# Zero matmuls ahead of the first tile, an earlier second tile, a later bias broadcast and a shorter scale chain in a gated layer kernel on one core

## The chip, the cores and the metric

The kernel runs on one core of a Trainium2 chip. The metric is the device time of one execution in microseconds (us), lower is better. Times given as "us" come from executions on the chip; positions such as "at 7.75" are microseconds from the start of the span of one profiled execution.

## What is computed

For 1024 tokens (4 x 256) of width 512 the layer normalises each token, runs a gated projection in which half of the entries of each row are dropped, runs a mixture of experts with a shared expert, and multiplies the two:

```
xn = layernorm(x)                                  # 1024 x 512, eps 1e-5
s  = silu(xn @ w_gate.T)                           # 1024 x 1376
s[the 688 entries of smallest |s| in each row] = 0
s  = (s * (xn @ w_up.T)) @ w_down.T                # 1024 x 512
logits = xn @ router_w + router_b                  # 16 experts in 4 groups
scores = softmax(logits) + router_bias             # best 2 groups, then best 2 experts
y  = sum over chosen experts of score * ((silu(xn@w1+b1) * (xn@w2+b2)) @ w3 + b3)
z  = (silu(xn@sw1+sb1) * (xn@sw2+sb2)) @ sw3 + sb3 # the shared expert, inner width 256
out = x + s * silu(y + z)
```

All data are float32.

## The kernel before, in words

The entry function runs `quick_path` and, only if a flag is set at its end, `general_path`. The profile is of an execution that ran `quick_path` alone, so only that one matters here.

Tokens are cut into 8 tiles of 128, one token per partition. The 1376 columns of the gate and up projections are cut into three blocks (512, 512 and 352; `COLS`), the 512 of the contraction into four chunks of 128. In the trace each matmul call of float32 data appears as two MATMUL instructions and two weight loads, so one block of one tile (four chunks) is eight instructions.

The start of `quick_path`, which the change touches, goes as follows:

- SP, the queue for plain loads, issues tile 0 of x (`load_x`, L516), then the four row chunks of the first block of gate weights (L527), then tiles 1, 2 and 3 of x, then the other two blocks of gate weights (L531) and the router weights (L532). Tiles 4 to 7 follow in a later loop; they reuse the four buffers of tag "x", so each waits until an earlier tile was normalised. After them come the shared expert's weights (L940, L941) and the up weights (L946).
- POOL builds the identity matrix for the transposes and issues four loads on its own queue: router bias terms, the experts' bias columns, and `b3s_sb` (L544), the shared expert's output bias, 512 values broadcast to 128 partitions. It is read by `finish` at L890, first at 149.3.
- `stats(t0, n)` handles n tiles on VectorE (DVE). Per tile it takes BATCH_NORM_STATS (L568) and its aggregation (L569); then, for all n tiles at once, it forms the reciprocal square root: add eps (L574), two integer instructions for a first guess (L576, L577), and three Newton steps of four small instructions each (L580 to L583). Below, "scale chain" means L574 to L583, fifteen instructions, each needing the one before it.
- `normalise(t0, n)` writes `xn` (DVE, L588), transposes it on TensorE in four chunks into `pt` (L593), and ScalarE copies `pt` to `xnT` (L594).
- `gate(t, k)` multiplies `xnT` of tile t by column block k (L608) into `pz`; ScalarE applies silu (L615).

The program calls these for tile 0, for tile 1, and for tiles 2 and 3 together:

```
for t, n in ((0, 1), (1, 1), (2, 2)):
    stats(t, n)
    normalise(t, n)
    for j in range(t, t + n):
        gate(j, 0)
```

The order of instructions on each engine is not that of the text: a planner in the framework takes them by priority, which follows the program, but fills an engine's gaps with later instructions that it believes to be ready by its own estimate of times. In the trace VectorE starts its instructions in the order of its list, so one placed early whose data come late holds up what stands behind it.

After the start come the other gate blocks, the search for each row's median magnitude (DVE and ScalarE), the choice of experts, the shared expert, the up projection, the fetched experts, and per tile `finish`: expert outputs, transposes of s, the down projection (L921), product and residual.

Of the kernel before, what the change touches and what calls it, by code (L numbers as in the profile page):

```python
# [9 lines left out]
F32 = mybir.dt.float32  # L10
# [4 lines left out]
ALU = mybir.AluOpType  # L15
# [4 lines left out]
P = 128  # L20
H = 512
# [7 lines left out]
E = 16  # L29
# [452 lines left out]
def quick_path(  # L482
# [15 lines left out]
    nc = tc.nc  # L498
    NT = N_TOK // P

    const = ctx.enter_context(tc.tile_pool(name="const", bufs=1))
# [8 lines left out]
    def psum(name):  # L510
        return ps.tile([P, 512], F32, tag="mm", name=name)


    def load_x(t, again=""):
        xt = work.tile([P, H], F32, tag="x", name=f"x{again}{t}", bufs=4)
        nc.sync.dma_start(xt, x[ts(t, P), :])  # L516
        return xt
# [6 lines left out]
    X = {0: load_x(0)}  # L524
    lo, n = COLS[0]
    for c in range(HC):
        nc.sync.dma_start(wg_sb[:, c, :n], wg[ts(c, P), :n])  # L527
    for t in range(1, 4):
        X[t] = load_x(t)
    for lo, n in COLS[1:]:  # L530
        nc.sync.dma_start(wg_sb[:, :, lo : lo + n], wg_v[:, :, lo : lo + n])  # L531
    nc.sync.dma_start(wg_sb[:, :, I:], rw)  # L532


    ident = const.tile([P, P], F32, tag="ident", name="ident")
# [4 lines left out]
    nc.gpsimd.dma_start(rbias_sb, rbias.partition_broadcast(P))  # L540
    bcols_sb = const.tile([P, 2 * NCH], F32, tag="bcols", name="bcols_sb")
    nc.gpsimd.dma_start(bcols_sb, bcols)
    b3s_sb = const.tile([P, H], F32, tag="b3s", name="b3s_sb")
    nc.gpsimd.dma_start(b3s_sb, b3[E].partition_broadcast(P))  # L544
    ones = const.tile([P, P], F32, tag="ones", name="ones")
    nc.gpsimd.memset(ones, 1.0)

# [17 lines left out]
    def stats(t0, n):  # L565
        for t in range(t0, t0 + n):
            st = small.tile([P, 6], F32, tag="st", name=f"st{t}")
            nc.vector.bn_stats(st, X[t])  # L568
            nc.vector.bn_aggr(mv[:, t, :], st)  # L569


        r = rstd[:, t0 : t0 + n]
        ve = small.tile([P, n], F32, tag="ve", name=f"ve{t0}")
        nc.vector.tensor_single_scalar(ve, mv[:, t0 : t0 + n, 1], EPS, ALU.add)  # L574
        ri = r.bitcast(I32)
        nc.vector.tensor_single_scalar(ri, ve.bitcast(I32), 1, ALU.logical_shift_right)  # L576
        nc.vector.tensor_scalar(ri, ri, -1.0, float(0x5F3759DF), ALU.mult, ALU.add)  # L577
        q = small.tile([P, n], F32, tag="q", name=f"q{t0}")
        for _ in range(3):
            nc.vector.tensor_mul(q, r, r)  # L580
            nc.vector.tensor_mul(q, q, ve)
            nc.vector.tensor_scalar(q, q, -0.5, 1.5, ALU.mult, ALU.add)
            nc.vector.tensor_mul(r, r, q)  # L583

# [345 lines left out]
# [4 lines that stand above are left out]
            gate(j, 0)  # L934
    for t in range(4, NT):
        X[t] = load_x(t)
    shared = []
    for e in range(E, NCH):
        w = expert_tiles(f"shared{e}")
# [5 lines left out]
    for lo, n in COLS:  # L945
        nc.sync.dma_start(wu_sb[:, :, lo : lo + n], wu_v[:, :, lo : lo + n])  # L946
    stats(4, 4)
    for k in range(1, 3):
        for t in range(4):
# [53 lines left out]
def swiglu_topk_gated_by_moe_kernel(  # L1003
    tc: tile.TileContext,
    x: bass.AP,
    wg: bass.AP,
    wu: bass.AP,
    wd: bass.AP,
    wexp: bass.AP,
    bcols: bass.AP,  # L1010
    b3: bass.AP,
    rw: bass.AP,
    rb: bass.AP,
    rbias: bass.AP,
    out: bass.AP,
):
    nc = tc.nc
    args = (x, wg, wu, wd, wexp, bcols, b3, rw, rb, rbias, out)
    with ExitStack() as keep:
        pool = keep.enter_context(tc.tile_pool(name="flag", bufs=1))  # L1020
        flag = pool.tile([P, 1], I32, tag="flag", name="flag")
        quick_path(tc, *args, flag)
        v = nc.values_load(flag[0:1, 0:1], min_val=0, max_val=1)
        with tc.If(v > 0):
            general_path(tc, *args)
# [64 lines left out]
```

## Time and profile before

| what | us |
|---|---|
| median of 3 runs | 346.92 |
| lowest and highest | 346.51, 347.85 |
| profiled execution, its own time | 346.43 |
| its span in the trace | 344.6 |

| engine | busy us, share of the span |
|---|---|
| TensorE matmul (PE) | 327.0, 95% |
| TensorE weight load (PEld) | 161.2, 47% |
| VectorE (DVE) | 158.7, 46% |
| ScalarE (ACT) | 90.7, 26% |
| GpSimd (POOL) | 22.3, 6% |

The profiled execution took 1.83 us more than its span; that lies outside what the trace shows. "Busy" counts an engine's instructions from start to end; matmuls overlap one another, so their sum of means can exceed their busy time. In the timeline a row gives the start, the time from the first instruction's start to the last one's end, the engine, the line, what is written and read, the count, and in brackets the idle time before it with the instruction or load that ended it.

### The profile page before, as it was taken

To read this page: it belongs to the slowest core of one execution; us is meant where nothing else is said; L and a number is where in the kernel's file an instruction comes from. 1 tells how busy PE (TensorE), PEld (TensorE's weight loads), DVE (VectorE), ACT (ScalarE), POOL (GpSimd) and SP (SyncE) were. 2 spreads that over 40 slices of the span, in tenths; PEclk is the share of its full clock that TensorE was granted. 3 is DMA by queue.
4 is the path that set the end of the run, shared out by engine and by line. 5 is a ranking of instruction groups with operands and counts; after the bars stand their busy time and mean duration, and the time that the engine had idled before them with its cause. 6 is when DMAs were issued, how large, how long until landed. Compare 5 with 4: busy or idle time off the path is not lost.

```text
span 344.6 us, 2574 instructions
## 1 busy us (share of the span) xinstructions
PE 327.0 (95%) x898; PEld 161.2 (47%) x898; DVE 158.7 (46%) x353; ACT 90.7 (26%) x149; POOL 22.3 (6%) x30
## 2 busy tenths in 40 slices
PE   1899999999999999999999999999999999999991
PEld 0344465444444444445454444454454544544480
DVE  4752005999978323987983300123150431504300
ACT  1322169861169787000000010020120201202010
POOL 4000000000000000460000000001010010110100
PEclk9999999999999999999999999999999999999997
DMA  6989002000090000160000000000010110000000
GB/s 193 324 307 355 2 0 61 0 1 2 2 320 6 0 0 2 39 187 18 0 0 2 0 0 1 0 2 34 27 61 0 63 50 11 30 0 30 33 19 22
DMA packets 10165, 18.99 MB, mean 55 GB/s; under 512 B 1360, under 2 KB 2688, under 8 KB 10144
## 3 DMA queue, kind: packets, MB, share of 16 engines
q1 hardware_dynamic: 9328, 16.35, 13.6%
q0 software_dynamic: 816, 2.39, 2.6%
q8 instruction: 9, 0.15, 0.2%
q14 instruction: 12, 0.10, 0.1%
HBM read 16.65 MB, written 2.10 MB: 54 GB/s over the span
## 4 chain that ended last, share of the span: by engine, by line
PE 92%; DMA 2%; DVE 2%; ACT 1%; SPq 1%; issue 0%
PE po L921 22%; PE pu L846 21%; PE pz L608 21%; PE pys L881 4%; PE pbr L863 4%; PE par L863 4%; PE pbs L863 4%; PE pas L863 4%; PE pyr L881 4%; PE ps L905 3%; DMA x<-in_x_dram 2%; SPq L527 0%; ACT xnT L594 0%; ACT a L621 0%; DVE st L568 0%; ACT s L615 0%
## 5 line engine op out<-in xcount | busy, mean ns | idle before, releaser
L608 PE MATMUL pz<-wg_sb,xnT 128*128 128x512 f32 (+1 forms) x192 | 78.7, 571 | 1.7 <-ACT xnT L594 1.6
L921 PE MATMUL po<-wd_sb,sT 128*128 128x512 f32 (+3 forms) x198 | 77.7, 549 | 0.0
L846 PE MATMUL pu<-wu_sb,xnT 128*128 128x512 f32 (+1 forms) x192 | 74.2, 548 | 0.0
L608 PEld LDWEIGHTS pz<-wg_sb,xnT 128*128 128x128 f32 x192 | 37.2, 196 | 41.4 <-issue 31.3
L846 PEld LDWEIGHTS pu<-wu_sb,xnT 128*128 128x128 f32 x192 | 36.4, 190 | 37.4 <-issue 29.7
L921 PEld LDWEIGHTS po<-wd_sb,sT 128*128 128x128 f32 (+1 forms) x198 | 37.0, 190 | 36.1 <-issue 33.5
L924 DVE TENSOR_TENSOR g<-po,g 128x512 f32<-128x512 f32 (+1 forms) x9 | 5.7, 632 | 70.5 <-PE po L921 70.5
L653 ACT ACTIVATE ja<-a,c 128x1376 bf16<-128x1376 f32 x24 | 34.6, 1440 | 6.3 <-DVE c L666 5.9
L907 ACT COPY sT<-ps 128x512 f32<-128x512 f32 (+1 forms) x24 | 11.5, 516 | 92.9 <-PE ps L905 92.9
L615 ACT ACTIVATE s<-pz 128x512 f32<-128x512 f32 (+1 forms) x24 | 13.1, 547 | 44.1 <-PE pz L608 44.1
L870 ACT ACTIVATE hr<-par,bs 128x512 f32<-128x512 f32 x4 | 2.8, 688 | 80.9 <-PE par L863 80.9
L853 DVE TENSOR_TENSOR s<-s,pu 128x512 f32<-128x512 f32 (+1 forms) x24 | 14.6, 626 | 10.9 <-PE pu L846 10.9
L926 POOL TENSOR_TENSOR g<-g,xr 128x512 f32<-128x512 f32 x7 | 8.8, 1263 | 162.3 <-DVE g L924 162.3
L881 PE MATMUL pys<-w3shared,hs 128*128 128x512 f32 x32 | 15.1, 595 | 0.0
L881 PE MATMUL pyr<-w3slot,hr 128*128 128x512 f32 x32 | 15.0, 592 | 0.0
L863 PE MATMUL pas<-xnT,w12shared 128*128 128x512 f32 x32 | 14.4, 592 | 0.0
L863 PE MATMUL pbs<-xnT,w12shared 128*128 128x512 f32 x32 | 14.4, 592 | 0.0
L863 PE MATMUL par<-xnT,w12slot 128*128 128x512 f32 x32 | 14.4, 592 | 0.0
L863 PE MATMUL pbr<-xnT,w12slot 128*128 128x512 f32 x32 | 14.4, 592 | 0.0
L871 DVE SCALAR_TENSOR_TENSOR hr<-pbr,bs,hr 128x512 f32<-128x512 f32 x4 | 3.0, 750 | 23.1 <-PE pbr L863 23.1
L648 DVE TENSOR_SCALAR_CACHE_REDUCE jd<-a,c 128x1376 bf16<-128x1376 f32 x8 | 13.2, 1646 | 0.2
L679 DVE SCALAR_TENSOR_TENSOR w<-a,c 128x1376 f32<-128x1376 f32 x8 | 13.2, 1648 | 0.1
(124 smaller groups left out, 235.9 us busy)
## 6 DMA issues: line engine op xcount, KB each, us to landing
wd_sb<-in_wd_dram SPq DMA_DIRECT2D x1, 2560.0 KB, 10.5
x<-in_x_dram SPq DMA_DIRECT2D x8, 256.0 KB, 5.7
wu_sb<-in_wu_dram SPq DMA_DIRECT2D x2, 1024.0 KB, 9.7
xr<-in_x_dram SPq DMA_DIRECT2D x8, 256.0 KB, 2.8
out_dram<-g SPq DMA_DIRECT2D x7, 256.0 KB, 2.0
wg_sb<-in_wg_dram SPq DMA_DIRECT2D x4, 256.0 KB, 5.8
wg_sb<-in_wg_dram SPq DMA_DIRECT2D x1, 1024.0 KB, 9.8
w12shared<-in_wexp_dram SPq DMA_DIRECT2D x2, 512.0 KB, 5.5
```

Of the source, the lines that this page charges most:

```text
L608: nc.tensor.matmul(pz[:, :w], xnT[:, c, ts(t, P)], wg_sb[:, c, lo : lo + w], start=(c == 0), stop=(c == HC - 1),)
L615: nc.scalar.activation(S[t][:, lo : lo + n], pz[:, :n], AF.Silu)
L648: nc.vector.tensor_scalar(junk, A[t0 + i], c, None, ALU.is_lt, ALU.add, accum_out=cnt)
L653: nc.scalar.activation(junk, A[t0 + i], AF.Sign, bias=c, scale=-1.0, accum_out=cnt)
L679: nc.vector.scalar_tensor_tensor(w, A[t0 + i], self.c[:, i : i + 1], A[t0 + i], ALU.is_lt, ALU.mult)
L846: nc.tensor.matmul(pu[:, :n], xnT[:, c, ts(t, P)], wu_sb[:, c, lo : lo + n], start=(c == 0), stop=(c == HC - 1),)
L853: nc.vector.tensor_mul(S[t][:, lo : lo + n], S[t][:, lo : lo + n], pu[:, :n])
L863: nc.tensor.matmul(pk, w[0][:, k * H + c * P : k * H + (c + 1) * P], xnT[:, c, cols], start=(c == 0), stop=(c == HC - 1),)
L881: nc.tensor.matmul(py, h[:, ts(t, P)], w, start=(i == 0), stop=(i == len(which) - 1))
L905: nc.tensor.transpose(pt[:w, ts(c - c0, P)], s[:, c * P : c * P + w], ident)
L907: nc.scalar.copy(sT[:, c0 : c0 + full, :], pt[:, : full * P].rearrange("p (c n) -> p c n", c=full),)
L921: nc.tensor.matmul(po, sT[:w, c, :], wd_sb[:w, c, cols], start=(c == 0), stop=(c == IC - 1))
```

## The change

Four edits, all in `quick_path`. A 128 x 512 tile of zeros is set on VectorE, and TensorE multiplies it by itself in four calls (three of 512 columns, one of 256) whose result is read by nobody. The load of x tile 1 moves from behind the fourth chunk of the first gate block to behind its second. The load of `b3s_sb` moves from POOL's queue at the start to SP's queue behind the loads of tiles 4 to 7. Where `stats` handles one tile (tiles 0 and 1), each Newton step forms r*ve*r in one instruction with `ve` as per-partition scalar, in place of two multiplications.

```
     for c in range(HC):
         nc.sync.dma_start(wg_sb[:, c, :n], wg[ts(c, P), :n])
-    for t in range(1, 4):
+        if c == 1:
+            X[1] = load_x(1)
+    for t in range(2, 4):
         X[t] = load_x(t)
     for lo, n in COLS[1:]:
         nc.sync.dma_start(wg_sb[:, :, lo : lo + n], wg_v[:, :, lo : lo + n])
     nc.sync.dma_start(wg_sb[:, :, I:], rw)
+
+    zeros = const.tile([P, 512], F32, tag="zeros", name="zeros")
+    nc.vector.memset(zeros, 0.0)
+    pw = psum("pw")
+    for n in (512, 512, 512, 256):
+        nc.tensor.matmul(pw[:, :n], zeros[:, :P], zeros[:, :n], start=True, stop=True)
...
-    b3s_sb = const.tile([P, H], F32, tag="b3s", name="b3s_sb")
-    nc.gpsimd.dma_start(b3s_sb, b3[E].partition_broadcast(P))
...
         for _ in range(3):
-            nc.vector.tensor_mul(q, r, r)
-            nc.vector.tensor_mul(q, q, ve)
+            if n == 1:
+                nc.vector.scalar_tensor_tensor(q, r, ve, r, ALU.mult, ALU.mult)
+            else:
+                nc.vector.tensor_mul(q, r, r)
+                nc.vector.tensor_mul(q, q, ve)
             nc.vector.tensor_scalar(q, q, -0.5, 1.5, ALU.mult, ALU.add)
             nc.vector.tensor_mul(r, r, q)
...
     for t in range(4, NT):
         X[t] = load_x(t)
+    b3s_sb = const.tile([P, H], F32, tag="b3s", name="b3s_sb")
+    nc.sync.dma_start(b3s_sb, b3[E].partition_broadcast(P))
     shared = []
```

## The prediction, made before the changed kernel ran

> **What bounds the kernel now.** I read the page first, engine shares and slices:
>
> ```profile
> PE 327.0 (95%) x898; PEld 161.2 (47%) x898; DVE 158.7 (46%) x353; ACT 90.7 (26%) x149; POOL 22.3 (6%) x30
> ...
> PE   1899999999999999999999999999999999999991
> ...
> PEclk9999999999999999999999999999999999999997
> ```
>
> PE is full from the third slice (17.2 us) on. Only the first two slices, 0 to 17 us, and the tail have room. Next the waits of PE, all of them:
>
> ```profile
> PE pt L593 <- DVE xn L588: 8.4, 3, 7.7
> PE pz L608 <- ACT xnT L594: 1.6, 3, 0.7
> ```
>
> Over the whole span PE waits 10 us, 7.7 of it ahead of the first transposes; from 22 us on the same view gives only 0.4 + 0.3. So what the start gains moves everything behind it, provided that nothing behind waits for a load. Third, the timeline of the start (start, duration, engine, line):
>
> ```profile
> 7.05 0.55 DVE L588 TENSOR_SCALAR xn<-x,mv,rstd 128x512 f32<-128x512 f32 x1
> 7.75 1.08 PE L593 MATMUL pt<-ident,xn 128*128 128x128 f32 x4 [7.75 <-DVE xn L588]
> 9.51 6.61 PE L608 MATMUL pz<-wg_sb,xnT 128*128 128x512 f32 x8 [0.68 <-ACT xnT L594]
> 9.94 0.69 DVE L568 BATCH_NORM_STATS2 st<-x 128x6 f32<-128x512 f32 x1 [2.34 <-DMA x<-in_x_dram]
> 11.70 0.69 DVE L568 BATCH_NORM_STATS2 st<-x 128x6 f32<-128x512 f32 x1 [0.84 <-DMA x<-in_x_dram]
> 12.31 0.14 DVE L574 TENSOR_SCALAR ve<-mv 128x1 f32<-128x1 f32 x1
> 13.94 0.33 PEld L608 LDWEIGHTS pz<-wg_sb,xnT 128*128 128x128 f32 x1 [0.52 <-issue]
> 14.79 0.33 PEld L608 LDWEIGHTS pz<-wg_sb,xnT 128*128 128x128 f32 x1 [0.52 <-issue]
> 15.52 0.59 PE L608 MATMUL pz<-wg_sb,xnT 128*128 128x512 f32 x1
> 15.76 0.54 DVE L588 TENSOR_SCALAR xn<-x,mv,rstd 128x512 f32<-128x512 f32 x1
> 16.36 0.66 PE L593 MATMUL pt<-ident,xn 128*128 128x128 f32 x4 [0.25 <-DVE xn L588]
> 17.70 3.70 PE L608 MATMUL pz<-wg_sb,xnT 128*128 128x512 f32 x8 [0.68 <-ACT xnT L594]
> 18.66 0.19 PEld L608 LDWEIGHTS pz<-wg_sb,xnT 128*128 128x128 f32 x1 [0.24 <-issue]
> 19.09 0.19 PEld L608 LDWEIGHTS pz<-wg_sb,xnT 128*128 128x128 f32 x1 [0.24 <-issue]
> 22.56 7.99 PE L608 MATMUL pz<-wg_sb,xnT 128*128 128x512 f32 x18 [0.29 <-ACT xnT L594]
> ```
>
> Two things stand here. The same eight matmuls take 6.61 us for tile 0 and 3.70 for tile 1: weight loads come every 0.85 us in the first and every 0.43 in the second. The step between the last two matmuls of tile 0 is 0.73 (about 14.79 to 15.52), which puts the change of pace at about 15.4, 5.9 us after steady matmuls began. The clock row shows full clock all along, so it doesn't show this. And tile 1's normalised data are ready at 16.30, just after tile 0's gate block ends at 16.12: two chains end together. Tile 1's is late because its scale chain (12.31) stands behind the statistics of tile 2 (11.70), whose load lands then. Last, the loads:
>
> ```profile
> x<-in_x_dram SPq DMA_DIRECT2D x1, 256.0 KB, 6.8
> ...
> wg_sb<-in_wg_dram SPq DMA_DIRECT2D x4, 256.0 KB, 5.8
> ...
> b3s_sb<-in_b_dram POOLq DMA_DIRECT2D x1, 256.0 KB, 8.0
> ```
>
> Tile 1 of x is issued at 3.07 and lands 6.8 later, at 9.9; the four weight chunks ahead of it take 5.8 in the median.
>
> **The change part by part.** *Shorter chain.* Three instructions of tile 0's chain go, 0.19 us from start to start; the joined one costs what the rows of that kind on 128x4 do (0.16, against 0.15 for a multiplication). 3 x 0.19 = 0.57, so xn of tile 0 ends at 7.60 - 0.57 = 7.03. A per-partition scalar might cost more: the nearest small row with one takes 0.22, which leaves 0.39. I take 0.57.
>
> *Zeros.* No VectorE fill is in the trace. Between POOL's 128x128 one at 0.20 and four times that, 0.80, I take 0.54, that of VectorE's 128x512 instruction. From 0.74, where other engines begin, it ends at 1.28; PE starts about 0.15 later (7.60 to 7.75), at 1.43. Four calls are eight matmul instructions: six of 512 columns at 0.855 and two of 256 at half of that, 5.13 + 0.86 = 5.99, end 7.42. VectorE waits for x until 3.24 anyway, so the fill costs nothing; if it began only at 3 us, the zeros would end near 9.7 and hold the transposes 2.5 us. As the pace rose after 5.9 us of steady matmuls, it would rise at 7.3. The transposes start at 7.45 instead of 7.75, take 0.66 instead of 1.08, and the first gate block starts 0.68 later, at 8.8. At full pace PE is ready for tile 1's transposes 3.53 later (17.70 to 21.23 now), at 12.3, against 16.1.
>
> [...]
>
> *Tile 1 earlier.* It is issued in the place of the third chunk, at 2.12, and by the chunks' 5.8 lands at about 7.9, against 9.9; the two chunks behind it land about where it landed, by 9.9, and are wanted at 8.8 + 4 x 0.43 = 10.5 and 11.4. So they have cover of 0.6 us or more; each us that they are later than that costs one. Tile 0's row from landing to xn took 7.60 - 3.24 = 4.36, less 0.57 is 3.79: uninterrupted, tile 1 is ready at 11.7, before PE at 12.3. But the planner puts the statistics of tiles 2 and 3 into gaps of that chain. Tile 2 keeps its place in the queue (11.67). If they stand at the chain's end with a few steps behind them: 11.7 + 0.69 + four steps of 0.19 + 0.55 = 13.7; with tile 3's (12.56) too, at most 14.3. Since tile 1 now starts two loads ahead of tile 2 more than before, most of its chain should be done by then. Between 12.3 and 14.3 I take 13.1 for the transposes.
>
> *Bias later.* One 256 KB load leaves POOL's queue; b3s is next read at 149.3, over 100 us after it can land, so its later issue (one more of about 0.4 on SP ahead of the shared weights, read from 93) is covered. With 0.8 us less to move (256 KB at the 324 GB/s of the second slice) tiles 1 and 2 may land up to 0.8 earlier; I count nothing for it, but keep it in the range. POOL only reaches its fills sooner.
>
> *What is late next.* From tile 1's transposes to the gate block of tile 2 is now 22.56 - 16.36 = 6.20. It stays if tiles 2 and 3 are normalised in time: tile 3 needs 12.56 + 0.69 + fifteen steps of 0.2 + 1.1 = 17.4, PE asks for it near 13.1 + 4.9 = 18. The second gate weight block was issued at 5.17 and landed 9.8 later, at 15; it is wanted near 26.
>
> *Sum.* 16.36 - 13.1 = 3.3 us off the whole: 346.43 becomes 343.1 for an execution like the profiled one. The median lies 0.49 above that execution, so I forecast 346.92 - 3.3 = 343.6. Best case, transposes at 12.3 or a little before: a gain of 4.1, and 0.4 for the spread of the runs, 342.4.
>
> **The rivals.** *A: tile 2 still gates tile 1 (0.12).* If the planner leaves the order as it is, the chain starts after 11.70 + 0.69 and xn comes at 16.30 less 0.4 to 0.9. PE is free at 12.3 and waits instead. For it: this is the order that the timeline shows. Against it: tile 1 now has three loads' distance from tile 2, not one. Gain 0.4 to 0.9: 346.3.
>
> *B: the zeros don't hold the pace (0.08).* Then the first block starts at 9.2 and takes 6.6, ends 15.8, tile 1's transposes 0.5 earlier than now: 346.4. Zeros might not count as work, or the gap before real work may undo it; nothing in the trace excludes either.
>
> *C: tile 1's statistics stand within tile 0's chain (0.14).* With tile 1 two loads closer to tile 0, the planner may take it for landed before tile 0 is done. VectorE then waits for the load in the middle of the first chain: 7.9 + 0.69 + four steps of 0.19 + 0.55 = 9.9 in place of 7.03. If the pace survives the 2.5 us of idle PE, the first block starts at 11.3 and PE is ready for tile 1 at 14.8: gain 1.5, 345.4.
>
> *D, slower: as C, and the pace falls back (0.10).* The first block starts at 9.9 + 0.15 + 1.08 + 0.68 = 11.8 and takes 6.6: tile 1's transposes at 18.4, 2.1 later than now: 349.0. It decides as soon as xn of tile 0 ends later than 7.6, and passes half a per cent from about 9.3 on. For it: VectorE's order, in which a late load stops a chain (11.70). Against it: that no PE gap in this trace was seen to lower the pace, and that tile 0's chain has nothing foreign in it now.
>
> **How the numbers follow.** The forecast has 0.56, A 0.12, B 0.08, C 0.14, D 0.10. About half a per cent (1.7 us) is what a measurement of this kernel can tell from no change. Faster by more: the forecast and some of C (0.06), 0.62. Within: A, B and the rest of C, 0.28. Slower: D, 0.10. The range takes the forecast with both ends (342.4 to 345.1), C, A and B: 342.4 to 346.4; D stays out.
>
> **What would show it.** Right: matmuls from about 1.4 to 7.4, transposes of tile 0 near 7.4, weight loads 0.43 apart in the first gate block, its eight matmuls near 3.7, tile 1's transposes near 13 and tile 2's gate block near 19.3, and from there the same pace. A shows as statistics of tile 2 ahead of L574 of tile 1; B as 0.85 spacing; C and D as a third statistics row ahead of tile 0's xn. Wrong altogether if PE shows a new wait behind 22 us.

## The result, and the profile after

The changed kernel takes as long as the one before: median 347.06 us over 22 runs (344.89 to 348.55) against 346.91 over 22 runs (345.97 to 348.93). The ratio is 1.0002, 95% interval 0.9985 to 1.0019. The forecast was 343.6.

The page of the changed kernel, in the same parts as that of the kernel before. Its profiled execution took 347.04 us.

```profile
span 345.2 us, 2583 instructions
...
PE 332.5 (96%) x906; PEld 163.5 (47%) x906; DVE 159.1 (46%) x348; ACT 90.7 (26%) x149; POOL 21.8 (6%) x29
...
PE   7789999999999999999999999999999999999992
...
PEclk9699999999999999999999999999999999999998
```

PE works from the first slice on, as intended, and that by itself gains nothing: the added busy time is zeros. New is the 6 in the clock row. In the kernel before no such dip stood at the start. The waits of PE, all of them:

```profile
PE pt L603 <- DVE rstd L584: 2.4, 1, 2.4
PE pz L618 <- ACT xnT L604: 1.7, 3, 0.7
PE pw L541 <- DVE zeros L538: 1.5, 1, 1.5
PE pt L603 <- DVE xn L598: 0.4, 1, 0.4
```

The first transposes still wait, now 2.4 us behind the zeros. (The view names the last VectorE instruction that the wait could match; by time it is tile 0's xn.) The timeline says why:

```profile
1.47 6.12 PE L541 MATMUL pw<-zeros 128*128 128x512 f32 x8 [1.47 <-DVE zeros L538]
...
5.87 0.16 DVE L593 TENSOR_TENSOR rstd<-rstd,q 128x1 f32<-128x1 f32 x1
...
8.07 0.69 DVE L575 BATCH_NORM_STATS2 st<-x 128x6 f32<-128x512 f32 x1 [2.04 <-DMA x<-in_x_dram]
8.68 0.20 DVE L588 SCALAR_TENSOR_TENSOR q<-rstd,ve 128x1 f32<-128x1 f32 x1
...
9.30 0.55 DVE L598 TENSOR_SCALAR xn<-x,mv,rstd 128x512 f32<-128x512 f32 x1
...
9.99 0.63 PE L603 MATMUL pt<-ident,xn 128*128 128x128 f32 x4 [2.41 <-DVE rstd L584]
...
11.29 6.75 PE L618 MATMUL pz<-wg_sb,xnT 128*128 128x512 f32 x8 [0.68 <-ACT xnT L604]
...
17.88 0.60 PE L603 MATMUL pt<-ident,xn 128*128 128x128 f32 x4
...
24.07 8.42 PE L618 MATMUL pz<-wg_sb,xnT 128*128 128x512 f32 x19 [0.29 <-ACT xnT L604]
```

After two of tile 0's three Newton steps (5.87 + 0.16) VectorE's list holds tile 1's statistics. Tile 1 lands at about 8.0, VectorE stands still for 2.04 us, and the third step follows at 8.68: tile 0's xn ends at 9.85 instead of 7.60 before. That is rival C. And the first gate block takes 6.75 us although the transposes just ahead of it ran at the full pace (0.63): the pace rose and fell again, rival D. The windows of this execution (time, busy of PE, PEld, DVE, ACT, POOL, then granted clock) show the fall:

```profile
9.00:10.00 1.00, 0.01 (x1) 0.04 (x1) 0.96 (x7) 0.00 (x0) 0.00 (x0) 1.00 1.07 414
10.00:11.00 1.00, 0.62 (x4) 0.38 (x4) 0.90 (x5) 0.34 (x1) 0.00 (x0) 0.82 1.03 391
11.00:12.00 1.00, 0.70 (x1) 0.50 (x2) 1.00 (x5) 0.98 (x2) 0.00 (x0) 0.50 1.07 388
...
17.00:18.00 1.00, 1.00 (x4) 0.28 (x3) 0.00 (x0) 0.00 (x0) 0.00 (x0) 0.77 0.58 127
```

A mean of 0.82 over 10 to 11 puts the fall at 10.64, 3.05 us after the last zero matmul ended (7.59); 0.77 over 17 to 18 puts the rise at 17.46. Half pace lasted 6.8 us.

Tile 2's first gate block, from which PE is full, starts at 24.07 instead of 22.56: 1.5 later, where 3.3 earlier was forecast. The span is only 0.6 longer, because the rest of the program, from that block to the end of the span, takes 345.2 - 24.07 = 321.1 instead of 344.6 - 22.56 = 322.0. That gain of 0.9 lies behind the last output (issued at 338.09 before, 6.5 us ahead of the end, and at 339.60 now, 5.6 ahead) and is taken up below.

By their mean clock, not all executions lose the pace. Of the 22, four had a mean granted clock of 0.993 or more and took 344.89 to 346.04 (median 345.45), five lay at 0.988 or 0.989 (median 346.65), and thirteen at 0.985 or less (median 347.49). The four of the highest clock lie where rival C had put them (345.4), though C had not reckoned with the shorter end.

### The profile page after: what moved, and what is told of

It reads as the page before. It is cut to its first block, busy times and chain, and to the rows that moved or that the text cites. A ratio compares the mean times of both kernels' runs of the same rounds, so it can differ in the third digit from the quotient of the medians.

```text
span 345.2 us, 2583 instructions
## 1 busy us (share of the span) xinstructions
PE 332.5 (96%) x906; PEld 163.5 (47%) x906; DVE 159.1 (46%) x348; ACT 90.7 (26%) x149; POOL 21.8 (6%) x29
## 4 chain that ended last, share of the span: by engine, by line
PE 94%; DMA 2%; ACT 1%; DVE 1%; SPq 0%; issue 0%
PE pz L618 23%; PE po L931 22%; PE pu L856 21%; PE pys L891 4%; PE pbr L873 4%; PE pas L873 4%; PE pbs L873 4%; PE par L873 4%; PE pyr L891 4%; PE ps L915 3%; DMA x<-in_x_dram 2%; ACT xnT L604 1%; ACT s L625 0%; ACT a L631 0%; SPq L527 0%; DVE st L575 0%
## 5 line engine op out<-in xcount | busy, mean ns | idle before, releaser
L627 DVE TENSOR_TENSOR lg<-pz,rb_sb 128x16 f32<-128x16 f32 x8 | 1.4, 172 | 27.4 <-ACT s L625 27.4
```

## The experiments

The theory: each edit does about what it says, but the early load changes VectorE's order, which stops tile 0's chain, and the stop lets the pace fall. Each was timed beside the kernel before. "Block 2" is tile 2's first gate block, and the last two columns are of each one's profiled execution.

| run | median us | ratio to before (95%) | block 2 at | block 2 to end |
|---|---|---|---|---|
| pin_both | 341.88 | 0.9854 (0.9838 to 0.9871) | 19.41 | 321.1 |
| pin_first | 345.04 | 0.9952 (0.9931 to 0.9974) | 20.88 | 321.0 |
| second_tile_back | 346.08 | 0.9979 (0.9958 to 1.0001) | 21.92 | 320.7 |
| zeros_longer | 346.18 | 0.9975 (0.9954 to 0.9995) | 20.56 | 321.1 |
| pin_no_zeros | 344.34 | 0.9920 (0.9892 to 0.9949) | 21.88 | 321.0 |
| zeros_alone | 349.24 | 1.0059 (1.0038 to 1.0080) | 25.95 | 322.0 |
| no_zeros | 347.67 | 1.0020 (0.9998 to 1.0042) | 25.42 | 321.0 |
| early_alone | 348.65 | 1.0056 (1.0033 to 1.0080) | 24.80 | 322.0 |
| bias_alone | 346.13 | 0.9972 (0.9957 to 0.9988) | 21.78 | 321.9 |
| pin_bias_front | 342.61 | 0.9880 (0.9846 to 0.9915) | 20.02 | 321.1 |
| pin_long_chain | 342.60 | 0.9876 (0.9843 to 0.9908) | 20.83 | 320.8 |
| pin_early_more | 341.76 | 0.9846 (0.9821 to 0.9871) | 19.03 | 321.0 |

**VectorE's order pinned (pin_both, pin_first).** The framework can tie a block's instructions to come behind a given one on the same engine, in order of issue alone (`normalise` now returns its last xn instruction; pin_first has `(1, -1)` in the condition, so that only t = 1 is tied):

```
+    done = None
     for t, n in ((0, 1), (1, 1), (2, 2)):
-        stats(t, n)
-        normalise(t, n)
+        if t in (1, 2, -1):
+            with tc.issue_after(done.ins):
+                stats(t, n)
+        else:
+            stats(t, n)
+        done = normalise(t, n)
...
```

> The changed kernel, with VectorE's order alone pinned: the statistics of tile 1 are issued behind tile 0's xn, those of tiles 2 and 3 behind tile 1's xn. Theory (the order costs the gain: tile 1's statistics inside tile 0's chain make VectorE wait for a load, PE idles 2.4 us, and the pace falls back): tile 0's xn ends at 7.25 (5.87 + 0.19 + 0.64 + 0.55) instead of 9.85, transposes at 7.6 right behind the zeros, first gate block from 8.95 with weight loads 0.43 apart, tile 1's xn at 12.0 (8.05 + 3.97), tile 2's gate block at 18.8 instead of 24.07 and, before the change, 22.56: 3.8 us below the kernel before, 343.1. Rival (zeros do not raise or hold the pace whatever the order): first gate block at 9.4 with loads 0.85 apart, 6.7 long, tile 2's gate block near 22.2: 346.6.

> The changed kernel with only the first pin: tile 1's statistics behind tile 0's xn; those of tiles 2 and 3 stay free, and the planner then puts them ahead of most of tile 1's scale chain. Theory: first gate block as with both pins (8.95 to 12.5), but VectorE waits for tile 2's load (10.6) and tile 1's xn comes near 14.8, so PE idles 2.3 us there; tile 2's gate block at 21.1, 345.4. Rival (order of tiles 2 and 3 does not matter since PE is the bound there): as with both pins, 343.1.

The timeline of pin_both:

```profile
1.47 5.13 PE L541 MATMUL pw<-zeros 128*128 128x512 f32 x8 [1.47 <-DVE zeros L538]
7.72 0.63 PE L603 MATMUL pt<-ident,xn 128*128 128x128 f32 x4 [1.13 <-DVE xn L598]
9.03 3.70 PE L619 MATMUL pz<-wg_sb,xnT 128*128 128x512 f32 x8 [0.67 <-ACT xnT L604]
13.03 0.66 PE L603 MATMUL pt<-ident,xn 128*128 128x128 f32 x4 [0.30 <-DVE xn L598]
...
19.41 11.00 PE L619 MATMUL pz<-wg_sb,xnT 128*128 128x512 f32 x25 [0.22 <-ACT xnT L604]
```

With nothing but the order changed, the first gate block starts at 9.03 and takes 3.70, tile 1's transposes come at 13.03, and the kernel is 1.46% faster than before (1.29 to 1.62%): 4.9 us (3.8 expected), with 0.9 of it at the end of the program. That the forecast had put these transposes at 13.1 is luck in part: it reckoned with tile 2's statistics inside tile 1's chain, and here that chain runs uninterrupted from a landing at 9.00 (forecast 7.9). In pin_first the statistics of tiles 2 and 3 stand in tile 1's chain:

```profile
11.00 0.69 DVE L575 BATCH_NORM_STATS2 st<-x 128x6 f32<-128x512 f32 x1 [0.56 <-DMA x<-in_x_dram]
...
11.83 0.66 DVE L575 BATCH_NORM_STATS2 st<-x 128x6 f32<-128x512 f32 x1
...
14.69 0.66 PE L603 MATMUL pt<-ident,xn 128*128 128x128 f32 x4 [1.95 <-DVE xn L598]
```

PE idles 1.95 us there (2.3 expected), and tile 1's transposes come 1.7 later than in pin_both. This execution kept the pace; nine of the twelve of pin_first had a clock of 0.992 or less, against 0.995 and 0.996 in its three fastest. So both orders matter, and the rivals of both runs fall.

**The early load undone, and the early load alone (second_tile_back, early_alone).** The first puts tile 1's load back behind the fourth weight chunk in the changed kernel. The second moves it in the kernel before:

```
     for c in range(HC):
         nc.sync.dma_start(wg_sb[:, c, :n], wg[ts(c, P), :n])
+        if c == 1:
+            X[1] = load_x(1)
-    for t in range(1, 4):
+    for t in range(2, 4):
         X[t] = load_x(t)
```

> The changed kernel with one edit undone: the load of x tile 1 back behind the fourth weight chunk. Zeros, later bias load and shorter chain stay; the planner then leaves tile 0's chain alone. Theory: tile 0's xn at 7.25, first gate block from 8.95 at the full pace, PE free at 12.5, but tile 1's xn only at 15.3 to 15.9 as before, less the shorter chain; PE idles 3 us. If the pace survives that, tile 2's gate block comes at 21.7 and the time is 346.0; if it falls there, tile 1's block takes 6.6 and the time is 347.5 or more. Rival (the early load is what pays, and the order does no harm): slower than the changed kernel by about 1.

> The kernel before with nothing but the load of x tile 1 moved behind the second weight chunk; the planner then puts its statistics inside tile 0's chain, with five of the chain's instructions behind them. Theory (this edit alone is what costs): tile 0's xn at 10.2 instead of 7.6, first gate block at half pace from 12.1 to 18.7, tile 1's transposes at 18.7 instead of 16.4, 349.0. Rival (an earlier tile 1 helps, as it was the later of the two chains): 346.5 or below.

In early_alone the profile shows the stop by itself:

```profile
8.36 0.69 DVE L570 BATCH_NORM_STATS2 st<-x 128x6 f32<-128x512 f32 x1 [2.01 <-DMA x<-in_x_dram]
...
9.94 0.54 DVE L590 TENSOR_SCALAR xn<-x,mv,rstd 128x512 f32<-128x512 f32 x1
...
12.39 6.38 PE L610 MATMUL pz<-wg_sb,xnT 128*128 128x512 f32 x8 [0.68 <-ACT xnT L596]
```

xn ends at 10.48 (expected 10.2), the gate block starts at 12.39 and the time is 348.65 (expected 349.0): this edit alone costs 0.56%. Undone in the changed kernel it leaves 346.08, which the intervals set apart neither from the changed kernel nor from the one before (the rival had it slower by about 1), with tile 1's chain again behind tile 2's load; PE waits 1.86 us for it (14.18), and in that execution tile 1's gate block takes 5.25.

**The zeros: alone, left out, and longer.** zeros_alone adds only their lines to the kernel before, no_zeros and pin_no_zeros take them from the changed and the pinned kernel, and zeros_longer adds three calls:

```
-    for n in (512, 512, 512, 256):
+    for n in (512, 512, 512, 512, 512, 512, 256):
```

> The kernel before with nothing but the zeros added; VectorE's order and the loads as before. Theory (two chains ended together before, so the pace alone buys nothing): first gate block from 9.1 to 12.6 at full pace, tile 1's xn still at 16.3, PE idle 3.7 us: 346.8 if the pace survives that stretch, 347.5 to 349 on average since it often falls there. Rival (PE is the only bound): 3.2 us faster, 343.6.

> The changed kernel without the zeros; tile 1's statistics still stand inside tile 0's chain. Theory: tile 0's xn at about 9.9, first gate block from 11.8 at half pace to 18.4, tile 1 ready long before: tile 2's gate block near 24.4, 348.7, so the zeros bring about 1.6 to the changed kernel, in those executions in which the pace survives. Rival (the zeros do nothing for the changed kernel): 347.0, as the changed kernel.

> Both pins, early tile 1, later bias and shorter chain, but no zeros. Theory (the gain is the pace of the first gate block, and the order only lets it through): tile 0's xn at 7.6, transposes 1.08 at half pace, first gate block from 9.4 with loads 0.85 apart, end near 16.0, tile 1's xn ready at 13 and waiting for PE: tile 2's gate block at 22.2, 346.5, so the zeros are worth 4.6 of the pinned kernel's gain. Rival (the pins alone carry the gain): near 342.

> The changed kernel with three more calls of 512 columns of zeros, so that PE is busy until about 10 instead of 7.6; VectorE's order stays the changed kernel's, with tile 1's statistics inside tile 0's chain. Theory (the idle stretch lets the pace fall): weight loads of the first gate block 0.43 apart, block from 11.3 to 14.9, tile 2's gate block at 21.1, 345.4 in every run, so a smaller spread than the changed kernel's. Rival (the pace falls because transposes or the switch to other data end it, not idleness): first block still takes 6.7 and the time stays at 347.

zeros_alone is slower than before, a little more than the theory had it. Its timeline and windows:

```profile
9.31 3.70 PE L615 MATMUL pz<-wg_sb,xnT 128*128 128x512 f32 x8 [0.68 <-ACT xnT L601]
17.51 1.11 PE L600 MATMUL pt<-ident,xn 128*128 128x128 f32 x4 [4.50 <-DVE xn L595]
19.30 5.49 PE L615 MATMUL pz<-wg_sb,xnT 128*128 128x512 f32 x8 [0.67 <-ACT xnT L601]
```

```profile
15.00:16.00 1.00, 0.00 (x0) 0.00 (x0) 1.00 (x12) 0.00 (x0) 0.00 (x0) 1.00 0.88 252
16.00:17.00 1.00, 0.00 (x0) 0.00 (x0) 1.00 (x12) 0.00 (x0) 0.00 (x0) 0.55 0.22 73
```

The first block runs at the full pace, PE then waits 4.50 us for tile 1, the clock falls at 16.1, 3.1 us after PE stopped, and tile 1's transposes and block run slowly. The pace that was bought for tile 0 is paid back at tile 1. Not all of the wait comes from the zeros: in this execution tile 1's statistics began at 11.81 instead of 9.94, with the loads in the order of before, and its xn ended 1.15 later (17.45). Why the load landed later is open.

In zeros_longer PE has zeros until the late xn is there, and the profiled execution, the fastest of its twelve, is as expected:

```profile
1.47 8.26 PE L541 MATMUL pw<-zeros 128*128 128x512 f32 x14 [1.47 <-DVE zeros L538]
9.56 0.60 PE L603 MATMUL pt<-ident,xn 128*128 128x128 f32 x4
10.83 3.70 PE L618 MATMUL pz<-wg_sb,xnT 128*128 128x512 f32 x8 [0.67 <-ACT xnT L604]
```

So in this trace neither the transposes nor the change of data ended the pace, and PE kept busy kept it (granted clock 1.00 in every window up to 24 us). The expected smaller spread did not come: 343.54 to 347.49, with four of twelve executions at a clock below 0.99, and three at 346.4 to 346.8 with 0.993 or 0.994. No trace shows those executions, so what held them up stays open; tile 1's landing, which stops tile 0's chain in this kernel, moved between 7.4 here and 9.2 in no_zeros.

Without zeros the pinned kernel takes 344.34, against 341.88 with them: zeros are worth about 2.5 when the order is right. I had expected 4.6; 0.9 of that was the longer end of the kernel before, which pin_no_zeros does not have, and tile 2's gate block came at 21.88 instead of 22.2. In the changed kernel they bring 0.6 by the medians (347.67 less 347.06; 1.6 expected), which the intervals do not set apart from nothing. Of these differences 0.2 and 0.3 lie outside the span: the two kernels without zeros take 2.1 and 2.2 us there in the median, the two with them 1.9.

**The other two edits (bias_alone, pin_bias_front, pin_long_chain).** bias_alone moves only the load of `b3s_sb` in the kernel before; pin_bias_front moves it back in the pinned kernel; pin_long_chain restores the four-instruction Newton step there (edits as in the diff above).

> The kernel before with nothing but the bias load moved from POOL's queue at the start to SP's queue behind tiles 4 to 7. From the start of tile 2's first gate block to the end of the span the kernels so far take 322.0 us where the bias is loaded at the start (before, zeros_alone, early_alone) and 320.7 to 321.1 where it is loaded later. Theory: the moved load shortens that stretch by 1.0, and PE's start can gain at most 0.25 since tile 0's gate block ends at 16.1: 345.8. Rival (the difference at the end comes from something else in those kernels, and the moved load is worth nothing, as predicted): 346.8, and 322.0 in that stretch.

> The kernel with both pins, and the bias load back on POOL's queue at the start. Theory of the moved load: 1.0 slower than with both pins, 342.9, with 322 from tile 2's gate block to the end. Rival: 341.9, and 321.

> The kernel with both pins, and the scale chain of tiles 0 and 1 in its long form again (four instructions per Newton step). The joined instruction took 0.22 and its step 0.64 in the changed kernel, against 0.77 for the long step, so three steps save 0.39. Theory (both chains now stand on the path, one behind the other in part): tile 0's transposes 0.39 later, tile 1's too: 0.4 slower than with both pins, 342.3. Rival (the saving is hidden behind the zeros or the load of tile 1): 341.9.

The moved bias load is worth 0.8 (346.13 against 346.92; 0.4 to 1.5 by the interval) in the kernel before. In the pinned one moving it back costs 0.7 (342.61 against 341.88) with overlapping intervals, and 0.3 of that lies outside the span (2.2 us there, 1.9 in pin_both). My theory of it fell: block 2 to end is 321.9 in bias_alone and 321.1 in pin_bias_front, so it does not touch the end. The gain is at the start:

```profile
9.83 5.15 PE L606 MATMUL pz<-wg_sb,xnT 128*128 128x512 f32 x8 [0.68 <-ACT xnT L592]
10.95 0.66 DVE L566 BATCH_NORM_STATS2 st<-x 128x6 f32<-128x512 f32 x1
...
15.59 0.66 PE L591 MATMUL pt<-ident,xn 128*128 128x128 f32 x4 [0.60 <-DVE xn L586]
```

In bias_alone tile 2's statistics run at 10.95 instead of 11.70, with no wait, and tile 1's transposes at 15.59 instead of 16.36: 0.8 earlier. That is also what 256 KB take at 324 GB/s (the second slice of the page of before), but that this is the cause is not shown. In the same trace tile 1 landed no earlier than before (10.12 against 9.94), and the pace rose earlier, so that the first gate block took 5.15 us instead of 6.61; with 6.61 PE would have been free only at 16.44.

The shorter chain's worth is not set apart: pin_long_chain is 0.7 slower than pin_both, with overlapping intervals, where the rows give 0.39 per chain. Its profiled execution shows that the pinned order can lose the pace too:

```profile
8.10 0.63 PE L600 MATMUL pt<-ident,xn 128*128 128x128 f32 x4 [1.06 <-DVE xn L595]
9.40 5.40 PE L616 MATMUL pz<-wg_sb,xnT 128*128 128x512 f32 x8 [0.67 <-ACT xnT L601]
```

```profile
9.00:10.00 1.00, 0.60 (x1) 0.40 (x2) 0.86 (x5) 0.98 (x2) 0.00 (x0) 0.77 1.05 401
...
12.00:13.00 1.00, 1.00 (x3) 0.45 (x2) 0.93 (x4) 0.00 (x0) 0.00 (x0) 0.52 1.05 373
```

The zeros ended at 7.04 and PE idled 1.06 us, no more than in pin_both (1.13). Still the granted clock, 0.77 from 9 to 10 and 0.52 from 12 to 13, shows a fall at 9.54 and a rise at 12.96, and tile 2's gate block came 1.4 later than in pin_both.

**One place earlier (pin_early_more).** In the pinned kernel tile 1's load goes behind the first weight chunk (`c == 0`).

> The kernel with both pins, and the load of x tile 1 one place earlier still, behind the first weight chunk. With both pins tile 1's xn was ready 0.25 after PE was free for it. Theory: tile 1 lands up to 1 us earlier, PE's wait of 0.3 ahead of its transposes goes, and the second weight chunk still has time: 341.6. Rival (the second weight chunk, now behind 256 KB more, lands after the first gate block wants it): 342 or more, with a wait for the load in that block.

PE no longer waits for tile 1, whose transposes follow the gate block at 12.66, and 341.76 is the lowest median of all, but within the interval of pin_both.

## Why the prediction was wrong

The step that failed is "Tile 1 earlier". It took the planner's interleaving for tile 1's chain (transposes between 12.3 and 14.3) and let tile 0's chain run clean, with C and D at 0.24 together. The same early arrival that frees tile 1's chain also brings its statistics in among tile 0's, and C's own arithmetic held: 9.9 forecast for xn, 9.85 measured; first block 11.8 in D and 11.3 in C, measured 11.29; D's tile 1 transposes 18.4, measured 17.88. The order was the question, the prices were known, and the chance was put on the wrong order.

The forecast's own order would not have given the forecast either. pin_first has it: tile 0's chain is clean, and the planner sets the statistics of tiles 2 and 3 into tile 1's chain. There nine of that chain's twelve small instructions stand behind tile 2's statistics, where the forecast had four steps; tile 1 lands at 8.97 instead of 7.9; its xn ends at 14.63, where the forecast had 13.1 for the transposes and 14.3 at most; and the median is 345.04, with the low clock in most executions. pin_both also keeps tiles 2 and 3 out of tile 1's chain and ends at 341.88, below the forecast and below the range's low end of 342.4.

Why 347.06 and not D's 349.0: the end of the program is 0.9 shorter, tile 1's transposes come 0.5 earlier than D has them, and in some executions, by their mean clock, the pace survives.

The other terms:

- Zeros: start 1.47 (forecast 1.43), end 7.59 (7.42). Right. The pace did rise around their end, since the transposes at 9.99 took 0.63.
- Shorter chain: a step of 0.64 instead of 0.77 makes 0.39 over three steps, not 0.57. The joined instruction took 0.22, the other bound that the prediction named.
- Tile 1's landing: about 8.0 (7.9). Right in this trace; in the traces of the eight other kernels with this order of loads its statistics began between 7.4 and 9.6.
- Bias: counted at nothing, worth 0.8 by itself. The bound in the text had 0.8, but by an earlier landing of tiles 1 and 2, which is not shown.
- B, that zeros do not count as work, is refuted by the 3.70 of the first block in pin_both. A's mechanism is second_tile_back and pin_first: with tile 2's statistics ahead, PE waits 1.9 us.
- Two slips in the sums, which decide nothing: by D's own terms the loss passes half a per cent from an xn end of about 9.5 on, not 9.3, since in the kernel before tile 1's transposes wait 0.25 for their data; and transposes at 14.3 give 344.9, not 345.1.

After a fall, half pace lasted 6.8 us in the changed kernel (10.64 to 17.46), 6.8 in zeros_alone (16.10 to 22.92), 3.4 in second_tile_back (15.24 to 18.66) and 3.4 in pin_long_chain (9.54 to 12.96), the ends worked out from the means of the windows. The 3.4 us that end at these four falls held, in the same order, 1.0, 0.3, 1.1 and 1.7 us of PE's work, transposes counted. What decides a fall is not shown. One stretch of 3.4 us at half pace takes 1.7/345 = 0.005 off the mean clock, so the groups of the changed kernel's executions near 0.993, 0.989 and 0.984 would fit none, one and two such stretches. That is an estimate: only one execution of each kernel has a trace.

## What to carry to other kernels

Moving a load also moved the instructions that read it: the planner set tile 1's statistics into tile 0's chain, and VectorE stood still for 2.04 us in the middle of that more urgent chain until the load was there. Read the new order off the changed program, or pin it, before pricing anything else. The zeros paid where the next real work followed closely and the chain behind it was ready too (about 2.5 us in pin_both, where PE waited 1.13 us for tile 0 and 0.30 for tile 1); alone, with 4.50 us of wait for tile 1, they made the kernel slower by 0.6%. The pace fell after idle stretches of 1.06 (pin_long_chain), 1.86 (second_tile_back), 2.41 (the changed kernel) and 4.50 us (zeros_alone), and held through 1.13 (pin_both), 1.95 (pin_first) and 1.06 us (pin_bias_front). Several edits that each lose or gain little (early load alone 1.0056, zeros alone 1.0059, bias alone 0.9972) gave 0.9854 together once the order was right, so single trials of them would have thrown the gain away.

## What was not expected of the hardware

The granted clock is 1.00 from the start in the windows of before, the changed kernel and zeros_alone, though weight loads came 0.85 apart in the first gate block of before and in the zeros of the changed kernel, against 0.43 later; in these traces it shows only a fall after a rise. Here the first half-paced stretch was read from the spacing of the weight loads.

The end of the program takes 0.9 us longer in four of the fourteen kernels: before, zeros_alone, early_alone and bias_alone. In these the last wait of SP's queue is on PE's, 1.6 to 1.8 us, against 0.7 in the ten others. In before one packet more than in the changed kernel went over the queue that is named for instructions. The waits of SP's queue at the end, of before and then of the changed kernel:

```profile
SPq L1086 <- PEq L1086: 1.6, 2, 1.1
```

```profile
SPq L1098 <- PEq L1098: 0.7, 2, 0.5
```

And the line of that queue in the DMA part of the two pages, in the same order:

```profile
q14 instruction: 12, 0.10, 0.1%
```

```profile
q14 instruction: 11, 0.09, 0.1%
```

The split of wait and stretch is the same in all fourteen: 1.6 to 1.8 us with 321.9 to 322.0, or 0.7 with 320.7 to 321.1. In before a packet of that queue goes at 344.4, 0.2 us before the end of the span; in the changed kernel none goes in the last 1 us. What the packet carries, and whether it has to do with the longer end, is not shown, and which edit does it is open: of the three edits that were tried alone (zeros, early load, bias) none removed it, and none of the four brought it back when it was undone.
